# A graph-network layer on one core: two small elementwise steps move from VectorE to ScalarE

## The chip, the cores and the metric

The kernel runs on one core of one Trainium2 chip. The metric is device time in microseconds (us) of that core for one launch, the median of a few runs. A core has five engines with a queue of instructions each: TensorE (PE, with its weight loads shown apart as PEld), VectorE (DVE), ScalarE (ACT), GpSimd (POOL) and SyncE (SP, which here issues nearly all DMAs). An engine takes its own queue in order; a wait for another engine is a wait on a semaphore. Where an instruction has more waits than fit into it, the surplus stands before it in the queue as EVENT_SEMAPHORE instructions.

## The reference, cut to what matters

```python
# N = 12500 nodes, 412500 edges sorted by dst; idx_i = src, idx_j = dst
h   = maximum(layernorm(x), 0)
h1  = h @ W_in2f                                         # 128 -> 128
Wij = (ssp(f_ij @ W_f1 + b_f1) @ W_f2 + b_f2) * rcut[:, None]
agg = segment_sum(h1[idx_j] * Wij, idx_i)                # one message per edge
out = x + ssp(agg @ W_o1 + b_o1) @ W_o2 + b_o2           # ssp = softplus - log 2
```

The call of the inner function passes `src` as `idx_i` and `dst` as `idx_j`: rows are gathered by `dst`, which is sorted, and summed by `src`, which is not.

## The kernel before, in words

**Main loop.** The edges are cut into chunks of 512 (806 chunks of four tiles of 128 edges); four chunks make a group. One pass of the loop (`step(k)`) works on several chunks at once, each at another stage; the whole order of instructions is written out by hand under `tc.manual_schedule()`. For one chunk the stages are:

- `rows`: SP loads 32 rows of the node table near the chunk's first `dst` (L608).
- `hidden`, for two chunks at a time: TensorE makes the filter's first layer `z` (L653); ScalarE takes abs (L656), exp (L657) and, one step later, log (L662) of it; `hidden_end` on VectorE makes `r` from `z` and the log (L668).
- `bias` and `value`: ScalarE writes the second layer's bias over a PSUM bank `v` (L757) and TensorE adds the second layer's products to it (L764, `start=False`).
- `window` and `pick`: VectorE compares to make the 0/1 matrix `at` (L744), and TensorE multiplies it with the loaded rows (L772); that is the gather. `picked`: ScalarE scales the result by the edge weights into `hg`, tile by tile (L780).
- `blocks`, `rank`, `rank_end`: VectorE (L673), TensorE (L692, L725) and VectorE again (L697) find a free slot in a DRAM table for every edge.
- `message`: VectorE multiplies `v` by `hg` into `o` (L791), and GpSimd scatters the four tiles of `o` into their slots by indirect DMAs (L795).

A row of `o` has 129 columns: 128 message values and, in the last column, the edge's place within its block of 128 nodes. `o` is a tile for two chunks (8 rows of 129 per partition), with four buffers. At every even chunk, before the product of that chunk, one VectorE instruction copies the 8 places per partition into the last column of both chunks (L789):

```python
if c % 2 == 0:
    kept["o"] = quad.tile([P, 2 * QT, RW], F32, name="o", bufs=4)
    w = min(2, self.n - c) * QT
    nc.vector.tensor_copy(kept["o"][:, :w, P], self.place[:, c * QT:c * QT + w])
```

As the first writer of a buffer that was used before, this copy carries the waits for the eight indirect DMAs that last read the buffer.

In an even step ScalarE's order is: bias `v` of chunk k+2 (which waits for the product L791 of chunk k, whose PSUM bank it takes), the four `hg` of chunk k+1, abs and exp for the pair k+4. In an odd step it is: bias `v`, four `hg`, log. VectorE's order in an even step is: `r` of the pair k+2 (which waits for the log of the step before), `at`, the copy of the places, the product L791, then the rank's reduction and the comparisons.

**Collecting.** The edges are in 7 segments with a slot table each. Behind the loop's front the slots of a finished segment are read back (`Collect`): SP loads them as `m` (L833, five buffers), VectorE compares the last column with 0..127 into `to` (L844), TensorE multiplies `m` by `to` and sums in PSUM (L857), and the sum is added to `agg` in SBUF (L878, L880). From about 2460 us on this runs beside the main loop.

**Tail.** The last segment is collected after the loop, and the output network runs with it, four blocks of nodes (a quad) at a time, 25 quads. `finish` is a generator with a stage per `yield`: 0, SP loads `x` into `xo` (L410, six buffers); 1, TensorE makes `z_out` (L414), ScalarE takes abs, relu, exp and log (L385, L386, L394, L395); 2, VectorE adds the two parts (`r_out`, L420) and adds `b_o2` to `xo` (L423); 3, TensorE makes the last product `v_out` (L427) in a PSUM bank of tag `v` (three buffers); 4, VectorE adds it to `xo` (L431); 5, SP stores `xo` (L434). While the quad q is collected, the quads q+1, q-1, q-2, q-3 and q-4 take one stage each, in that order. The same function also serves a fallback path that these inputs do not take.

Of the kernel before, what the change touches and what calls it, by code (L numbers as in the profile page):

```python
# [9 lines left out]
F32 = mybir.dt.float32  # L10
# [3 lines left out]
AF = mybir.ActivationFunctionType  # L14
# [3 lines left out]
P = 128  # L18
# [3 lines left out]
QT = CH // P  # L22
# [19 lines left out]
def gnn_kernel(  # L42
# [20 lines left out]
    nc = tc.nc  # L63
# [52 lines left out]
    def sbuf(name, shape, dtype=F32):  # L116
        return const.tile(shape, dtype, name=name)

    def spread(t, n):
        return t[:, None, :].to_broadcast([t.shape[0], n, P])  # L120
# [9 lines left out]
    for q in range(NQ):  # L130
        start = max(0, q * QN - NEAR)
        tables.append((start, (q + 1) * QN + NEAR + P - start))
    table_of = []
    for c in range(NC):
        n = c * CH * N // n_edges
# [4 lines left out]
    win, wf1, wf2, wo1, wo2 = (sbuf(n, [P, P]) for n in ("win", "wf1", "wf2", "wo1", "wo2"))  # L140
    bf1, nbf1, bo1 = (sbuf(n, [P, 1]) for n in ("bf1", "nbf1", "bo1"))
    bf2, bo2 = (sbuf(n, [P, P]) for n in ("bf2", "bo2"))
# [240 lines left out]
    def softplus_parts(a, r, z, bias):  # L383

        nc.scalar.activation(a, z, AF.Abs, bias=bias)  # L385
        nc.scalar.activation(r, z, AF.Relu, bias=bias)  # L386
# [6 lines left out]
    def softplus_logs(a):  # L393
        nc.scalar.activation(a, a, AF.Exp, scale=-1.0)  # L394
        nc.scalar.activation(a, a, AF.Ln, bias=half, scale=0.5)  # L395

    def finish(t0, n, sT, quad, psum):


        n0 = t0 * P  # L400
        full = min(n, N // P - t0)
        rest = N - n0 - full * P if full < n else 0
        xo = quad.tile([P, QT, P], F32, name="xo", bufs=6)
        pieces = []
        if full:
            pieces.append((P, slice(0, full), slice(n0, n0 + full * P)))
        if rest:
            pieces.append((rest, slice(full, n), slice(n0 + full * P, N)))
        for p, cs, rows in pieces:
            nc.sync.dma_start(xo[:p, cs, :], x[rows, :].rearrange("(c p) f -> p c f", p=p))  # L410
        yield

        z = psum.tile([P, 2, CH], F32, name="z_out", tag="z")[:, 0, :n * P]
        nc.tensor.matmul(z, wo1, sT, start=True, stop=True)  # L414
        a_n = quad.tile([P, 2, CH], F32, name="a_out", tag="a", bufs=2)[:, 0, :n * P]
        r_n = quad.tile([P, 2, CH], F32, name="r_out", tag="r", bufs=3)[:, 0, :n * P]
        softplus_parts(a_n, r_n, z, bo1)
        softplus_logs(a_n)
        yield
        nc.vector.tensor_add(r_n, r_n, a_n)  # L420
        for p, cs, rows in pieces:
            xi = xo[:p, cs, :]
            nc.vector.tensor_add(xi, xi, spread(bo2[:p, :], xi.shape[1]))  # L423
        yield
        v = psum.tile([P, QT, P], F32, name="v_out", tag="v", bufs=3)
        for i in range(n):
            nc.tensor.matmul(v[:, i, :], r_n[:, i * P:(i + 1) * P], wo2, start=True, stop=True)  # L427
        yield
        for p, cs, rows in pieces:
            xi = xo[:p, cs, :]  # L430
            nc.vector.tensor_add(xi, xi, v[:p, cs, :])  # L431
        yield
        for p, cs, rows in pieces:
            nc.sync.dma_start(out[rows, :].rearrange("(c p) f -> p c f", p=p), xo[:p, cs, :])  # L434


    def anyway(edge, quad, psum):
# [67 lines left out]
        for t0 in range(0, NTILE, QT):  # L505
            n = min(QT, NTILE - t0)
            o = quad.tile([P, QT, P], F32, name="s_out")
            nc.sync.dma_start(o[:, :n, :], sums[t0 * P:(t0 + n) * P, :].rearrange("(c p) f -> p c f", p=P))
            tps = psum.tile([P, QT, P], F32, name="t_out", tag="nodes")
            for i in range(n):  # L510
                nc.tensor.transpose(tps[:, i, :], o[:, i, :], ident)
            sT = quad.tile([P, QT, P], F32, name="sT")
            nc.scalar.activation(sT[:, :n, :], tps[:, :n, :], AF.Copy)
            for _ in finish(t0, n, sT[:, :n, :].rearrange("p c f -> p (c f)"), quad, psum):
                pass


    with tc.tile_pool(name="edge", bufs=2) as edge, tc.tile_pool(
        name="quad", bufs=3
# [3 lines left out]
        kept = {}  # L523
# [41 lines left out]
        class Group:  # L565
# [218 lines left out]
            def message(self, c, v, hg):  # L784

                if c % 2 == 0:
                    kept["o"] = quad.tile([P, 2 * QT, RW], F32, name="o", bufs=4)
                    w = min(2, self.n - c) * QT
                    nc.vector.tensor_copy(kept["o"][:, :w, P], self.place[:, c * QT:c * QT + w])  # L789
                o = kept["o"][:, c % 2 * QT:(c % 2 + 1) * QT, :]  # L790
                nc.vector.tensor_mul(o[:, :, :P], v, hg)  # L791
                views = self.seg.views
                for i in range(QT):
                    j = c * QT + i
                    put = nc.gpsimd.indirect_dma_start(  # L795
                        out=views[j % VIEWS],
                        out_offset=bass.IndirectOffsetOnAxis(ap=self.slot[:, j:j + 1], axis=0),
                        in_=o[:, i, :],
                        in_offset=None,
                    )  # L800
                    if i == 0 and self.g * NCHUNK + c == self.seg.cleared:
                        for name in self.seg.clears:
                            tc.add_manual_dep(
                                put.ins, name,
                                mybir.DependencyInfo(mybir.DependencyClass.Sync,
                                                     mybir.DependencyReason.DATA),
                                reason="cleared slots")
# [189 lines left out]
        t0, i = 0, 0  # L997
        while i < len(segs):

            j = max(range(i, len(segs)), key=lambda j: sum(todo[i:j + 1]) / (due[j] - t0))  # L1000
            n = sum(todo[i:j + 1])
            for m in range(n):
                zeros.setdefault(t0 + m * (due[j] - t0) // n, []).append(clears.pop(0))
            t0, i = due[j], j + 1
# [5 lines left out]
        while len(rate) < len(at):  # L1010
            n = len(at) - len(rate)
# [13 lines left out]
        i, k = 0, todo[0][0]  # L1025
# [43 lines left out]
        with tc.manual_schedule():  # L1069
# [49 lines left out]
            outs = []  # L1119
            for b in range(0, NBLK, QT):  # L1120
                n = min(QT, NBLK - b)
                sT = kept["agg"][:, b:b + n, :].rearrange("p c f -> p (c f)")
                outs.append(finish(b, n, sT, quad, psum))

            def go(q):
                if 0 <= q < NQ:
# [31 lines left out]
    with tc.If(missed > 0):  # L1158
        with tc.tile_pool(name="any_e", bufs=2) as edge, tc.tile_pool(
            name="any_q", bufs=2  # L1160
# [51 lines left out]
```

## Time and profile before

| | |
|---|---|
| runs of the kernel before | 5771.6, 5732.79, 5770.01 us; median 5770.01 |
| the profiled execution | 5772.48 us, of which 5770.8 us is the span of its instructions |
| mean granted TensorE clock | 0.718 of full speed; about 0.6 from 200 to 2500 us, about 0.8 from 2500 to 5620 us, 0.94 after |
| busy share of the span | PE 67%, DVE 59%, POOL 54%, ACT 47% |
| copy of the places (L789, DVE) | 403 instructions of 166 ns, 66.8 us |
| `b_o2` added to `xo` (L423, DVE) | 26 instructions, 16.9 us |
| main loop | from the start to about 5620 us |
| tail | about 5620 to 5765 us, then the last stores |

The busy shares are shares of the whole span and overlap each other; no engine is busy all the time. Durations of single instructions overlap with their neighbours on the same engine, so that the step from one start to the next is less than the duration. "Idle before" is the time in which an engine stood still ahead of an instruction, and after "<-" stands what ended it; "remote" means that the profile names no instruction for it, and "issue" that it shows no wait. The clock is the share of full speed that TensorE was granted.

### The profile page before, as it was taken

How to read it: one execution, taken by the hardware profiler on the slowest of the kernel's cores; microseconds unless marked ns; L12 is line 12 of the kernel's file. 1: busy time of each engine (PE TensorE's matmuls, PEld its weight loads, DVE VectorE, ACT ScalarE, POOL GpSimd, SP SyncE). 2: the span in 40 equal slices, each digit the busy share in tenths (PEclk: the TensorE clock that was granted, in tenths of full speed). 3: DMA queues.
4: the chain of work that ended last, by engine and by line, in shares of the span. 5: the costliest groups of instructions: out<-in, count | busy, mean ns of one | idle time of the engine just before them, and what ended most of it. 6: DMA issues, size and time to landing. Idle time of an engine off the chain costs nothing. (4 is left out here: it accounts for less than half of the span.)

```text
span 5770.8 us, 71871 instructions
## 1 busy us (share of the span) xinstructions
PE 3877.3 (67%) x21576; PEld 2912.2 (50%) x21576; DVE 3382.9 (59%) x6726; ACT 2715.3 (47%) x5490; POOL 3103.5 (54%) x3244
## 2 busy tenths in 40 slices
PE   5556555556555555577777777777777777777778
PEld 3333333333333333356655666566566665655557
DVE  5555555555444444466665666666666666566767
ACT  4455554555444444444444444444444444444444
POOL 5555555555555555555555555555555555555550
PEclk7665566565556566578777787788877788787879
DMA  5444443343333333255664554655555555555547
GB/s 150 138 135 141 130 141 119 115 137 104 99 89 87 106 109 87 82 152 161 188 183 137 158 160 144 190 163 157 160 168 173 154 150 178 165 141 153 145 126 215
DMA packets 515581, 820.80 MB, mean 142 GB/s; under 512 B 177074, under 2 KB 312870, under 8 KB 515186
## 3 DMA queue, kind: packets, MB, share of 16 engines
q1 hardware_dynamic: 411586, 602.85, 37.4%
q0 software_dynamic: 103168, 213.15, 11.2%
q8 instruction: 176, 2.88, 0.2%
q14 instruction: 219, 1.79, 0.1%
q10 hardware_dynamic: 432, 0.13, 0.0%
HBM read 419.09 MB, written 396.64 MB: 141 GB/s over the span
## 5 line engine op out<-in xcount | busy, mean ns | idle before, releaser
L795 POOL DMA_INDIRECT slots<-o,slot x3224 | 3100.3, 962 | 2522.6 <-DVE o L791 1605.2
L764 PE MATMUL v<-wf,r 128*128 128x128 f32 x6448 | 1209.4, 345 | 527.4 <-ACT a L657 207.3
L857 PEld LDWEIGHTS acc<-to,m 128*128 128x128 f32 x8132 | 1249.1, 238 | 577.1 <-issue 280.8
L857 PE MATMUL acc<-to,m 128*128 128x128 f32 x8132 | 1342.0, 329 | 271.0 <-DVE agg L880 136.4
L764 PEld LDWEIGHTS v<-wf,r 128*128 128x128 f32 x6448 | 1077.6, 251 | 850.7 <-issue 301.8
L780 ACT ACTIVATE hg<-picked,rcut 128x128 f32<-128x128 f32 x3224 | 913.1, 365 | 1256.6 <-remote 801.2
L697 DVE TENSOR_REDUCE top<-free 128x4 f32<-128x392 f32 x806 | 451.5, 560 | 1650.5 <-remote 990.2
L757 ACT ACTIVATE v<-bf 128x512 f32<-128x512 f32 x804 | 478.0, 595 | 1212.9 <-DVE o L791 888.5
L653 PE MATMUL z<-f,wf 20*128 20x512 f32 x1612 | 661.1, 881 | 406.9 <-DVE r L668 242.4
L844 DVE TENSOR_TENSOR to<-count_ps,m 128x512 f32<-128x512 f32 (+3 forms) x824 | 644.7, 806 | 255.3 <-remote 109.3
L772 PE MATMUL picked<-near,at 96*128 96x128 bf16 x3224 | 398.5, 257 | 495.3 <-ACT hg L780 317.4
L668 DVE SCALAR_TENSOR_TENSOR r<-z,nbf,a 128x1024 f32<-128x1024 f32 x403 | 516.2, 1281 | 242.3 <-ACT a L662 136.3
L656 ACT ACTIVATE a<-z,bf 128x1024 f32<-128x1024 f32 x403 | 454.0, 1127 | 400.4 <-remote 267.8
L772 PEld LDWEIGHTS <-at 96*128 96x128 bf16 x3224 | 315.5, 118 | 558.1 <-issue 531.3
L791 DVE TENSOR_TENSOR o<-v,hg 128x512 f32<-128x512 f32 x806 | 547.8, 680 | 16.8 <-ACT hg L780 12.8
L744 DVE TENSOR_TENSOR at<-count_ps,rel 96x512 bf16<-96x512 f32 x806 | 545.3, 677 | 0.0
L653 PEld LDWEIGHTS z<-f,wf 20*128 20x128 f32 x1612 | 174.6, 241 | 620.9 <-issue 428.9
L662 ACT ACTIVATE a<-a,half 128x1024 f32<-128x1024 f32 x403 | 468.1, 1162 | 0.0
L673 DVE TENSOR_TENSOR inb<-count_ps,blk 128x392 f16<-128x392 f32 x806 | 445.9, 554 | 0.0
L657 ACT ACTIVATE a<-a 128x1024 f32<-128x1024 f32 x403 | 425.8, 1057 | 12.8
L725 PE MATMUL free<-inb,rest_of 128*128 128x392 f16 x806 | 335.3, 416 | 117.6 <-issue 46.9
L692 PE MATMUL free<-inb,after 128*128 128x392 f16 x806 | 335.9, 417 | 17.4 <-issue 13.6
(108 smaller groups left out, 1142.5 us busy)
## 6 DMA issues: line engine op xcount, KB each, us to landing
m<-slots SPq DMA_DIRECT2D x311, 387.0 KB
m<-slots SPq DMA_DIRECT2D x317, 258.0 KB
rel<-rel_d SPq DMA_DIRECT2D x202, 384.0 KB
m<-slots SPq DMA_DIRECT2D x172, 322.5 KB
slots<-o,slot POOLq DMA_INDIRECT x3224
slots<-zero SPq DMA_DIRECT2D x96, 387.0 KB
slots<-zero SPq DMA_DIRECT2D x64, 516.0 KB
f<-in_f_t SPq DMA_DIRECT2D x404, 80.0 KB
```

The source lines that it names most:

```text
L653: nc.tensor.matmul(z[:, k, :], wf1[rows, :], self.f[rows, :], start=True, stop=True)
L662: nc.scalar.activation(a, a, AF.Ln, bias=half, scale=0.5)
L668: nc.vector.scalar_tensor_tensor(r, z, nbf1, a, op0=ALU.max, op1=ALU.add)
L744: nc.vector.tensor_tensor(at, prow_ps.to_broadcast([WP, CH]), self.rel[:, c, :], op=ALU.is_equal)
L757: nc.scalar.activation(v, spread(bf12, QT), AF.Copy)
L764: nc.tensor.matmul(v[:, i, :], r[:, i * P:(i + 1) * P], wf2, start=False, stop=True, skip_group_check=True)
L772: nc.tensor.matmul(ps[:, i, :], at[:, i * P:(i + 1) * P], near, start=i == 0, stop=i == QT - 1, skip_group_check=True)
L780: nc.scalar.activation(hg[:, i, :], ps[:, i, :], AF.Copy, scale=self.rcut[:, j:j + 1])
L791: nc.vector.tensor_mul(o[:, :, :P], v, hg)
L795: put = nc.gpsimd.indirect_dma_start(out=views[j % VIEWS], out_offset=bass.IndirectOffsetOnAxis(ap=self.slot[:, j:j + 1], axis=0), in_=o[: ...
L844: nc.vector.tensor_tensor(to[:, :n, :], count_ps[:, None, :].to_broadcast([P, n, P]), self.m[u][:, :n, P:].to_broadcast([P, n, P]), op=ALU ...
L857: nc.tensor.matmul(self.acc[b // QT][:, i, :], m[:, j, :P], to[:, j, :], start=t == 0, stop=t == self.seg.tiles(b) - 1)
```

## The change

The copy of the places into the last column of `o` becomes a ScalarE activation (a plain copy) at the same place of the source. In the tail, ScalarE writes `b_o2`, repeated for every node of the quad, over the PSUM bank `v_out` in stage 2, and the last product is added onto it (`start=False`); the VectorE addition of `b_o2` to `xo` is left out there. The bank is so taken one stage earlier. The fallback path keeps the old form (`seeded=False`).

```diff
-    def finish(t0, n, sT, quad, psum):
+    def finish(t0, n, sT, quad, psum, seeded=False):
...
         nc.vector.tensor_add(r_n, r_n, a_n)
-        for p, cs, rows in pieces:
-            xi = xo[:p, cs, :]
-            nc.vector.tensor_add(xi, xi, spread(bo2[:p, :], xi.shape[1]))
+        v = psum.tile([P, QT, P], F32, name="v_out", tag="v", bufs=3)
+        if seeded:
+            nc.scalar.activation(v[:, :n, :], spread(bo2, n), AF.Copy)
+        else:
+            for p, cs, rows in pieces:
+                xi = xo[:p, cs, :]
+                nc.vector.tensor_add(xi, xi, spread(bo2[:p, :], xi.shape[1]))
         yield
-        v = psum.tile([P, QT, P], F32, name="v_out", tag="v", bufs=3)
         for i in range(n):
-            nc.tensor.matmul(v[:, i, :], r_n[:, i * P:(i + 1) * P], wo2, start=True, stop=True)
+            nc.tensor.matmul(v[:, i, :], r_n[:, i * P:(i + 1) * P], wo2, start=not seeded,
+                             stop=True, skip_group_check=seeded)
...
                 if c % 2 == 0:
                     kept["o"] = quad.tile([P, 2 * QT, RW], F32, name="o", bufs=4)
                     w = min(2, self.n - c) * QT
-                    nc.vector.tensor_copy(kept["o"][:, :w, P], self.place[:, c * QT:c * QT + w])
+                    nc.scalar.activation(kept["o"][:, :w, P],
+                                         self.place[:, c * QT:c * QT + w], AF.Copy)
...
-                outs.append(finish(b, n, sT, quad, psum))
+                outs.append(finish(b, n, sT, quad, psum, seeded=True))
```

In the built program the order of instructions on TensorE, GpSimd and SyncE is the same as before. ScalarE has 403 copies more, 388 of them directly ahead of an even step's bias `v` (L757; 14 others have one evacuation, L878, between), and 25 writes of `v_out`. VectorE has these 403 and the 26 additions fewer. The waits for the eight indirect DMAs stand at ScalarE's copy now, and on VectorE they stand at the product L791 that follows. The first indirect DMA of a pair waits for ScalarE's copy as well as for the product, and the first `v_out` product of a quad waits for ScalarE's write.

## The prediction

> **What bounds the kernel now.** I read the page's shares first, then the waits, then the time line of two kinds of pair (two chunks, which share one log, one `r` and one tile `o`), then the tail.
>
> ```profile
> PE 3877.3 (67%) x21576; PEld 2912.2 (50%) x21576; DVE 3382.9 (59%) x6726; ACT 2715.3 (47%) x5490; POOL 3103.5 (54%) x3244
> PEclk7665566565556566578777787788877788787879
> ```
>
> No engine is busy all the time, so the main loop is set by a chain of waits. The clock row gives the granted TensorE clock in 40 slices: about 0.6 before collecting starts at 2460 us, about 0.8 after.
>
> ```profile
> POOL slots L795 <- DVE o L791: 1605.2, 358, 25.4
> DVE top L697 <- remote: 990.2, 163, 12.1
> ACT v L757 <- DVE o L791: 888.5, 325, 9.0
> ACT hg L780 <- remote: 801.2, 152, 10.2
> ```
>
> The columns are total us, times and longest. ScalarE's bias `v` waits 888 us for VectorE's product L791, and so does GpSimd (1605 us, so its scatters follow and do not lead). "remote" is a wait with no named releaser: VectorE and ScalarE stand there for rank and gather products of TensorE whose completion is signalled late. Pairing each rank reduction L697 with the recorded end of its product L692, 410 of 806 begin over 3 us after it, 2534 us in sum.
>
> ```profile
> 1799.26 1.16 ACT L662 ACTIVATE a<-a,half 128x1024 f32<-128x1024 f32 x1
> 1800.45 1.28 DVE L668 SCALAR_TENSOR_TENSOR r<-z,nbf,a 128x1024 f32<-128x1024 f32 x1 [2.35 <-issue]
> 1801.65 0.68 DVE L744 TENSOR_TENSOR at<-count_ps,rel 96x512 bf16<-96x512 f32 x1
> 1802.25 0.16 DVE L789 COPY o<-place 128x8 f32<-128x8 f32 x1
> 1802.32 0.68 DVE L791 TENSOR_TENSOR o<-v,hg 128x512 f32<-128x512 f32 x1
> 1803.04 0.60 ACT L757 ACTIVATE v<-bf 128x512 f32<-128x512 f32 x1 [2.62 <-issue]
> ```
>
> Columns: start, duration, engine, line, [idle before]. This is the end of a pair without a late TensorE signal. `r` starts 0.03 us after the log, `at` 1.20 later, the copy 0.60 later, the product 0.07 later, and the bias starts 0.04 us after the product ends, having stood idle 2.62 us. From the product at 1793.37 to the one at 1802.32 the starts on the chain differ by 0.71 (to bias), 0.54 (to `hg`), 1.00 (to abs), 1.16 (to exp), 0.96 (to bias), 0.52 (to `hg`), 1.00 (to log), 1.19 (to `r`), 1.20, 0.60 and 0.07: 8.95 us. By the starts of the 403 copies the mean pair takes 13.89 us; the fastest repeat this 8.95, many others before 2460 us take about 18.8, and in those the surplus of some 10 us is the "remote" wait.
>
> **The change, part by part.**
>
> ```profile
> L789 DVE COPY o<-place 128x8 f32<-128x8 f32 x403 | 66.8, 166 | 0.0
> L757 ACT ACTIVATE v<-bf 128x512 f32<-128x512 f32 x804 | 478.0, 595 | 1212.9 <-DVE o L791 888.5 <-issue 306.2 <-DVE at L744 17.1
> L333 ACT ACTIVATE rs<-rs 128x4 f32<-128x4 f32 x24 | 4.9, 205 | 0.8
> L423 DVE TENSOR_TENSOR xo<-xo,bo 128x512 f32<-128x512 f32 x24 | 16.4, 685 | 0.0
> ```
>
> (Count | busy us, mean ns | idle before.)
>
> *The copy leaves VectorE.* Its duration is 166 ns, 66.8 us in all, but the product starts 69 to 70 ns after the copy in all 403 cases, and `at` to copy is 597 ns, the same as `at` to product in odd steps. So the copy occupies 0.07 us of the chain: 403 x 0.07 = 28 us at most. The eight scatter waits move to the product behind `at`. They were surplus instructions of up to 50 ns, four to a copy, and the 597 ns show that they ran under `at`; there they still run. If that cover went, 4 x 0.05 = 0.2 us a pair, 80 us, would appear on VectorE; it does not go, since `at` stays ahead of them. The copy never found VectorE idle, so the buffers' scatters had always landed.
>
> *The copy joins ScalarE.* No row shows this shape on ScalarE. The nearest is L333, 128x4, at 205 ns; the far one is a bias, 595 ns. I take 0.2 us, plus four surplus waits at 38 ns (the median of those ahead of L357), 0.35 us. It stands ahead of the even step's bias (L757), and behind it wait the four `hg`, abs and exp, then TensorE's `value` and `z` products. Work that hides it: `r`, `at` and the product, 1.87 us from the start of `r` to that of the product, in which ScalarE waits anyway. By the trace's starts, ScalarE was idle 2.13 us or more ahead of 394 of 402 even biases. Cost 0. The other end, all of it exposed: 403 x 0.35 = 141 us.
>
> In the Trainium skill, ScalarE: Activation LUTs, section "Rules for kernel authors", speaks against the change: simple elementwise work (it names relu, max, min, add and mul) belongs on VectorE. The same page, section "What ACT_TABLE_LOAD costs", gives 186 ns + 0.833 ns per element, 193 ns here, close to the 205 ns row and to the biases' 595. By that rule, if ScalarE set the pace, the move would cost an estimated 403 x 0.19 = 77 us; the idle time ahead of the biases says that it costs nothing.
>
> *GpSimd.* The first scatter of a pair waits for the copy too, one surplus wait of 17 ns (median of the 832 there). The copy starts right after the log, over 1 us ahead of the product for which the scatter waits anyway: 403 x 0.017 = 7 us on GpSimd, beside 1605 us of idleness. Cost 0.
>
> *How much of the 28 us arrives.* `r` starts within 0.1 us of the log's end in 282 of 403 pairs, and the bias right after the product nearly always, so the 0.07 us reach ScalarE. What may swallow them is a late TensorE signal. If its lateness moves along with the work, all 28 us arrive. If it ends at a time of its own, only pairs without it gain: 145 of 402 pairs are under 12 us, 145 x 0.07 = 10 us. I take the middle, 19; with every wait set elsewhere it would be 0.
>
> *The tail.*
>
> ```profile
> 5677.12 0.69 DVE L880 TENSOR_TENSOR agg<-agg,acc 128x512 f32<-128x512 f32 x1
> 5677.73 0.69 DVE L420 TENSOR_TENSOR r_out<-r_out,a_out 128x512 f32<-128x512 f32 x1
> 5678.33 0.68 DVE L423 TENSOR_TENSOR xo<-xo,bo 128x512 f32<-128x512 f32 x1
> 5678.94 0.69 DVE L844 TENSOR_TENSOR to<-count_ps,m 128x512 f32<-128x512 f32 x1
> 5679.54 0.68 DVE L431 TENSOR_TENSOR xo<-xo,v_out 128x512 f32<-128x512 f32 x1
> 5680.13 0.68 DVE L844 TENSOR_TENSOR to<-count_ps,m 128x512 f32<-128x512 f32 x1
> ```
>
> One quad, 3.74 us from `agg` to `agg`: six VectorE instructions 0.60 apart, the third of them the `b_o2` addition that goes. TensorE's starts in the same quad: z to `v_out` 0.86, from there to the sum's sixteen products 0.89, and 1.99 for these, although eight take 0.90 where nothing waits: the second eight wait for the fourth VectorE row. Without the third row VectorE needs 3.14, and TensorE's own 0.86 + 0.89 + 2 x 0.90 = 3.55 decides: 0.19 less a quad, and over 24 quads at most 4.6 us. But from the seventh quad on SP holds the pace:
>
> ```profile
> SPq L410 <- DMA out<-xo: 39.0, 19, 4.4
> ```
>
> The load of `xo` waits for the store six quads before, and the loads of `m` queue behind it. SP's stores begin at 5688.08, 5691.91, 5696.15 and 5700.35, 4.1 us apart, more than VectorE's 3.74, and from 5714 us on VectorE waits for `m`. So only some five quads gain, 5 x 0.19 = 1 us. ScalarE's writes of `v_out` cost 25 x 0.6 = 15 us, at the price of the bias row (same shape, same bank type). Per quad ScalarE has 0.69 + 0.68 + 0.63 + 0.72 less overlap, 2.5 us of 3.74, so 0.6 fits in its wait for z. The bank was read by L431 an iteration earlier. In the drain after 5757 us nothing covers: log, then two writes (2 x 0.55) come ahead of the last products, while VectorE loses its two additions: the end moves by +1 us. If all 24 quads' gain came, and nothing in the drain, the tail would be 4.6 us shorter; if the writes lay open, 14 us longer. I take -1 + 1 = 0.
>
> **The sum.** Own time 5772.5 (span 5770.8 and 1.7 around it) - 19 + 0 = 5753.5. The median of the runs is 2.5 us lower than the profiled execution: 5751.
>
> **The rivals.**
>
> *Everything is swallowed.* The late signals decide; 28 us vanish in the waits for TensorE. For it: 2534 us of lateness and a mean pair of 13.89 against a chain of 8.95. Against it: the 8.95 and 18.8 us pairs contain the same tight piece from log to bias. Time: 5770, no change.
>
> *More late signals (slower).* Place: the rank and gather products; price: 2534 / 410 = 6.2 us each. The work on ScalarE and VectorE is re-timed by the change, and the alternation of 8.95 and 18.8 us pairs shows that the lateness depends on how the work falls. Five more late chunks of 806 (0.6%) eat the gain, and from 13 on the kernel is slower by over 1%; twenty (5% more) give 5751 + 124 = 5875, fourteen 5838. Against it: TensorE's, GpSimd's and SP's orders are the same, and nothing is added to TensorE. What makes the lateness I cannot name from this profile.
>
> *Fewer late signals.* The same lever the other way: ten fewer give 5751 - 62 = 5689.
>
> *ScalarE's copy lies open.* 141 - 28 = +113, 5883; it needs the 2.13 us of idleness to fall below 0.35. Nothing here does that.
>
> *It does not do what it says.* VectorE could still hold a wait for the copy; the built order shows none on the product.
>
> **How the numbers follow.** Most of the gain arrives: 0.50, at 5751, with its own range 5735 to 5768 (0 to 28 us, tail 5 either way). Swallowed: 0.23, 5755 to 5785. More late signals: 0.14; fewer: 0.10; open copy: 0.03. One per cent, 58 us, is about what a measurement of this kernel can tell from no change: its three runs lie 39 us apart. Faster by over 1% needs fewer late signals: 0.09. Slower by over 1% comes from most of the third case and the open copy: 0.14. Within 1%: 0.77. The range cuts off half of the two tail cases: 5700 to 5820.
>
> **What would show it.** The copy as 403 ScalarE rows of about 0.2 us with ScalarE still idle over 1.5 us between them and the even bias; `at` to product 0.60 us in even steps as in odd ones; fastest pairs of 8.88 us instead of 8.95; the `xo`, `bo` rows gone in the tail and its quads still near 3.6 to 4.2 us. I am wrong if the even bias no longer starts right at the product's end, if VectorE's product waits for scatters, or if the waits on "remote" and the count of late rank reductions move by more than 3%.

## The result, and the profile after

The changed kernel is slower: 5804.95 us median (5780.48 to 5821.42, 8 runs) against 5745.6 us for the kernel before (5704.52 to 5771.6, 8 runs). The ratio is 1.0102, its 95% interval 1.0077 to 1.0126. The forecast was a gain of some 0.3%. The profiled execution took 5803.15 us, 5801.4 of it span.

The busy shares and the clock row hardly move; VectorE has lost some 43 us of work and ScalarE has gained 55:

```profile
PE 3835.5 (66%) x21576; PEld 2881.8 (50%) x21576; DVE 3339.8 (58%) x6297; ACT 2769.9 (48%) x5918; POOL 3098.7 (53%) x3244
PEclk7565656656666555678777877778777787777879
```

The waits have the same heads, with one new name on the first (total us, times, longest):

```profile
POOL slots L801 <- ACT v L762: 1237.7, 265, 26.0
DVE top L702 <- remote: 951.5, 140, 12.3
ACT v L762 <- DVE o L797: 861.7, 330, 9.6
ACT hg L785 <- remote: 851.9, 144, 10.4
```

GpSimd's scatters seem to wait for ScalarE's bias. They do not: the wait they gained is for ScalarE's copy, which is over long before. The label goes by the last ScalarE instruction ahead of the scatter. The time line (start, duration, engine, line, [idle before]) of the end of a pair shows the chain as forecast:

```profile
1366.22 1.16 ACT L667 ACTIVATE a<-a,half 128x1024 f32<-128x1024 f32 x1
1367.26 0.22 ACT L794 ACTIVATE o<-place 128x8 f32<-128x8 f32 x1
1367.42 1.28 DVE L673 SCALAR_TENSOR_TENSOR r<-z,nbf,a 128x1024 f32<-128x1024 f32 x1 [0.59 <-ACT a L667]
1368.62 0.68 DVE L749 TENSOR_TENSOR at<-count_ps,rel 96x512 bf16<-96x512 f32 x1
1369.21 0.68 DVE L797 TENSOR_TENSOR o<-v,hg 128x512 f32<-128x512 f32 x1
1369.92 0.60 ACT L762 ACTIVATE v<-bf 128x512 f32<-128x512 f32 x1 [2.44 <-DVE o L797]
```

The copy (1367.26) sits right behind the log, `at` to product is 0.59 us with nothing between, and the bias starts 0.03 us after the product, having stood idle 2.44 us. The fastest pairs take 8.88 us. What is new stands in another pair, at the scatter:

```profile
1550.36 0.68 DVE L797 TENSOR_TENSOR o<-v,hg 128x512 f32<-128x512 f32 x1
...
1551.07 0.60 ACT L762 ACTIVATE v<-bf 128x512 f32<-128x512 f32 x1 [2.44 <-DVE o L797]
...
1551.78 0.96 POOL L801 DMA_INDIRECT slots<-o,slot  x1 [8.18 <-ACT v L762]
```

The same place in the kernel before:

```profile
1793.37 0.68 DVE L791 TENSOR_TENSOR o<-v,hg 128x512 f32<-128x512 f32 x1
...
1794.33 0.96 POOL L795 DMA_INDIRECT slots<-o,slot  x1 [7.72 <-DVE o L791]
```

After the change the product ends at 1551.04 and the first scatter starts at 1551.78, 0.74 us later; before, the product ends at 1794.05 and the scatter starts 0.28 us later. I call this distance the scatter lag. Its median in even chunks was 0.28 us before and is 0.75 us after; in odd chunks, whose first scatter has two waits as before, the shortest is 0.28 us in both kernels. In the built program the first scatter of a pair waits for an earlier scatter and for VectorE before, with VectorE's wait on the scatter itself; after, it has ScalarE's as a third, and VectorE's has moved into an EVENT_SEMAPHORE ahead of it, so that the scatter is taken up only when that has been resolved.

In the tail the `xo`, `bo` rows are gone and the quads are shorter where the forecast had them shorter:

```profile
5706.25 0.69 DVE L886 TENSOR_TENSOR agg<-agg,acc 128x512 f32<-128x512 f32 x1 [0.43 <-PE acc L863]
...
5708.07 0.69 DVE L436 TENSOR_TENSOR xo<-xo,v_out 128x512 f32<-128x512 f32 x1
...
5709.79 0.69 DVE L886 TENSOR_TENSOR agg<-agg,acc 128x512 f32<-128x512 f32 x1 [0.43 <-PE acc L863]
```

3.54 us from `agg` to `agg` instead of 3.74. The loss is in the main loop: up to the last product the profiled execution is 35 us longer than before.

### The profile page after: what moved, and what is told of

The parts are those of the page before. It is cut to its first block, busy times and chain, and to the rows that moved or that the text cites. A ratio compares the mean times of both kernels' runs of the same rounds, so it can differ in the third digit from the quotient of the medians.

```text
span 5801.4 us, 73471 instructions
## 1 busy us (share of the span) xinstructions
PE 3835.5 (66%) x21576; PEld 2881.8 (50%) x21576; DVE 3339.8 (58%) x6297; ACT 2769.9 (48%) x5918; POOL 3098.7 (53%) x3244
## 4 chain that ended last, share of the span: by engine, by line
## 5 line engine op out<-in xcount | busy, mean ns | idle before, releaser
L769 PE MATMUL v<-wf,r 128*128 128x128 f32 x6448 | 1196.5, 343 | 508.7 <-issue 181.8
L863 PEld LDWEIGHTS acc<-to,m 128*128 128x128 f32 x8132 | 1228.0, 235 | 608.4 <-issue 341.2
L863 PE MATMUL acc<-to,m 128*128 128x128 f32 x8132 | 1320.8, 325 | 306.4 <-issue 153.1
```

Of the source, the lines that this page charges most:

```text
L769: nc.tensor.matmul(v[:, i, :], r[:, i * P:(i + 1) * P], wf2, start=False, stop=True, skip_group_check=True)
L863: nc.tensor.matmul(self.acc[b // QT][:, i, :], m[:, j, :P], to[:, j, :], start=t == 0, stop=t == self.seg.tiles(b) - 1)
```

## The experiments

**What could do it.** Theory 1: the third wait delays GpSimd by 0.47 us per pair, and GpSimd's burst of scatters does lead. Theory 2: ScalarE's copy itself costs. Theory 3: with the chain 0.07 us shorter the work falls otherwise and TensorE's results come later. Theory 4: the tail's part costs. The runs came in five groups, on chips that the record numbers 5, 0, 15, 9 and 15 again. The kernel before took 4227 to 4234 us in the groups on 5 and 9 and in the second one on 15 (called condition B here), 5749 us in the group on 0 (condition A; it fits the first measurement), and 5820 us in the first group on 15 (condition C), 25 minutes before the second. So number 15 stands on both sides: that the chip makes the difference is not shown, and what sets the condition is open. The expectations below speak of chips where this text speaks of conditions. Ratios are to the kernel before in the same group.

### In condition B: nothing counts but GpSimd

Only the first part of the change, `places_only`:

```diff
-                    nc.vector.tensor_copy(kept["o"][:, :w, P], self.place[:, c * QT:c * QT + w])
+                    nc.scalar.activation(kept["o"][:, :w, P],
+                                         self.place[:, c * QT:c * QT + w], AF.Copy)
```

> Only the places move to ScalarE; the tail is as before. Theory 1 (the first scatter of a pair, which now has a third wait, starts 0.75 us after the product instead of 0.28, and GpSimd's burst sets the loop): scatter lag 0.75 us in even chunks, fastest pair 8.88 us, time 1.010 to 1.013 of before, that is about 5800 to 5820 us. Theory 2 (ScalarE's copy with its waits delays ScalarE): the same time, so this run does not tell 1 from 2. Theory 3 (the work is merely re-timed and TensorE's late signals fall otherwise): anything from 0.99 to 1.01. Theory 4 (the loss sits in the tail's new bank and ScalarE's writes): 0.995 to 1.000.

Only the second part, `bias_only` (the diff of `finish` and its call, with VectorE's copy kept):

> Only b_o2 goes into the PSUM bank; VectorE keeps the copy of the places. Theories 1, 2 and 3: scatter lag 0.28 us, fastest pair 8.95 us, tail after the last product some 4 us shorter, time 0.998 to 1.000 of before. Theory 4: 1.008 to 1.012.

The changed kernel with a wait more on VectorE, `product_waits`:

```diff
-                    nc.scalar.activation(kept["o"][:, :w, P],
+                    kept["placed"] = nc.scalar.activation(kept["o"][:, :w, P],
...
-                nc.vector.tensor_mul(o[:, :, :P], v, hg)
+                product = nc.vector.tensor_mul(o[:, :, :P], v, hg)
+                if c % 2 == 0:
+                    tc.add_manual_dep(product.ins, kept["placed"].ins.name, ...)
```

> As the changed kernel, but VectorE's even product also waits for ScalarE's copy (long done by then), so that the scatter behind the product no longer needs a wait of its own for it: two waits instead of three. Theory 1: scatter lag back at 0.28 us, fastest pair 8.88 us, time 0.993 to 0.998 of before, about 5710 to 5735 us, below both kernels. Theory 2: ScalarE's work is that of the changed kernel, so 1.008 to 1.012. Theory 3: no relation to the lag, 0.99 to 1.01; it is favoured if the lag is 0.28 us and the time still near 1.01.

The kernel before with the third wait alone, `third_wait`:

```diff
                     nc.vector.tensor_copy(kept["o"][:, :w, P], self.place[:, c * QT:c * QT + w])
+                    dummy = quad.tile([P, 2 * QT], F32, name="dummy", bufs=4)
+                    kept["placed"] = nc.scalar.activation(
+                        dummy[:, :w], self.place[:, c * QT:c * QT + w], AF.Copy)
...
+                    if i == 0 and c % 2 == 0:
+                        tc.add_manual_dep(put.ins, kept["placed"].ins.name, ...)
```

> As before (VectorE copies the places), with a ScalarE copy of the same size into a tile that nobody reads, for which the first scatter of a pair waits: three waits on it. Theory 1: scatter lag 0.75 us, fastest pair 8.95 us, time 1.010 to 1.018 of before, 5803 to 5850 us, since the 0.07 us on VectorE stay. Theory 2: the dummy copy carries no waits for scatters and lies in ScalarE's idle time, so 1.000 to 1.004. Theory 3: 0.99 to 1.01, with no order between the four runs by their scatter lag.

Measured: 0.9999 (0.9989 to 1.0008), 1.0005 (0.9996 to 1.0014), 0.9998 (0.9989 to 1.0007) and 1.0000 (0.9991 to 1.0009). None of the theories had reckoned with such a condition. The page of `places_only`:

```profile
PE 3371.5 (80%) x21576; PEld 2594.6 (61%) x21576; DVE 3347.3 (79%) x6323; ACT 2752.4 (65%) x5893; POOL 3105.6 (73%) x3244
PEclk8776767666666666589999999999999989999999
L796 POOL DMA_INDIRECT slots<-o,slot x3224 | 3102.5, 962 | 1011.6 <-issue 771.5
```

GpSimd's row has 1011.6 us of idle time, nearly all of it the 0.30 us behind each scatter; waits for products are at most 54 us of it. In the median GpSimd trails the products by 25 us. Its scatters start 1.266 us apart, 3224 x 1.266 = 4082 us, and that is the main loop; the mean pair takes 10.09 us, eight scatters. There the 0.07 us and the 0.47 us both lie behind GpSimd's backlog. Rank reductions for which VectorE stands idle over 1 us and that come over 3 us after the recorded end of their product do not occur in any profile of condition B; those of A and C have 222 to 252 each.

### In condition A: the third wait costs, and so does the change without it

> The changed kernel itself, beside the kernel before on the same chip. In the four runs above the kernel before took 4227 us, not 5746, and GpSimd trailed the products by 10 to 30 us: there GpSimd sets the loop with 3224 scatters 1.266 us apart, 4081 us. If this chip is like that one: 0.999 to 1.001, since a start that is 0.47 us late lies behind the backlog. If it is like the first one (GpSimd runs dry, the pairs alternate between some 9 and 19 us): 1.008 to 1.013, scatter lag 0.75 us in even chunks.

> As the run product_waits. On a chip where GpSimd never runs dry: 0.999 to 1.001. On a chip like the first one, theory 1 (the third wait): 0.993 to 0.998, scatter lag 0.28 us; theory 2 (ScalarE's copy): 1.008 to 1.012; theory 3 (re-timing): 0.99 to 1.01 without relation to the lag.

> As the run third_wait. On a chip where GpSimd never runs dry: 0.999 to 1.001. On a chip like the first one, theory 1: 1.010 to 1.018, scatter lag 0.75 us; theory 2: 1.000 to 1.004; theory 3: 0.99 to 1.01 without relation to the lag.

`pool_between` is the kernel before with a GpSimd instruction more, at the place where the first scatter has just been issued:

```diff
+                    if i == 0 and c % 2 == 0:
+                        idle = quad.tile([P, 64], F32, name="idle", bufs=4)
+                        nc.gpsimd.memset(idle, 0.0)
```

> As before, with one GpSimd memset of a 128x64 tile that nobody reads between the first and the second scatter of every pair, so GpSimd's burst is longer by the memset's step, estimated at 0.1 to 0.5 us. If GpSimd sets the loop (by its backlog, or on the first chip by what follows its burst), the time grows by 403 such steps, 40 to 200 us; the step is to be read from the trace and the growth divided by it. If GpSimd only follows, as the prediction had it: 0.999 to 1.001.

| run | ratio (95% interval) | scatter lag, even, median | fastest pair | first product to 177th even one | from there to the last even one |
|---|---|---|---|---|---|
| before (first measurement's profile) | 1 | 0.28 us | 8.95 us | 2387 us | 3198 us |
| after_again | 1.0109 (1.0075 to 1.0143) | 0.75 | 8.88 | 2414 | 3238 |
| product_waits_2 | 1.0092 (1.0063 to 1.0120) | 0.28 | 8.88 | 2376 | 3248 |
| third_wait_2 | 1.0152 (1.0122 to 1.0183) | 0.75 | 8.95 | 2433 | 3187 |
| pool_between | 1.0000 (0.9977 to 1.0022) | 0.28 | 8.95 | 2378 | 3191 |

The last two columns come from one profile each, and the executions of the kernel before differ by up to 67 us, so only their large differences count. (After's first profile has 2416 and 3202.)

`third_wait_2` bears out theory 1 in its size: 403 x 0.47 = 189 us of later starts, of which 1.5%, 87 us on 5749, reach the end. The profile shows the delay as time of the event semaphore (count, shortest/median/longest ns):

```profile
L798 POOLq EVENT_SEMAPHORE  x833: 17/43/16053, 29.3 to 5650.7; - x167
```

16 us is a wait for a product; in the kernel before the longest there was 43 ns, as it is in `product_waits_2`, whose scatter has two waits:

```profile
L795 POOLq EVENT_SEMAPHORE  x832: 17/17/43, 35.5 to 5614.4; - x167
L807 POOLq EVENT_SEMAPHORE  x832: 17/17/43, 35.3 to 5652.5; - x167
```

But `product_waits_2` is slow all the same. Theory 1 is true and not enough: with the third wait taken out, the changed kernel does not get measurably faster (1.0092 against 1.0109). Its two stages part company: up to the 177th pair, about where collecting begins, it is as fast as before or faster (2376); what it loses, it loses after.

Why GpSimd counts at all shows in the pairs. Before collecting, pairs of 8.95 and of some 18.8 us alternate, and two such pairs have a nearly fixed length together (I say that they lock): 27.77 us for the two before, 27.64 in `product_waits_2`, but 28.15 and 28.12 in the two profiles of after and 28.18 in `third_wait_2`. The two pairs with one late start of GpSimd in them are 0.4 to 0.5 us longer, the 0.47 us of the lag. After collecting begins a second pattern is frequent, single pairs of about 16.4 us. One of `product_waits_2` (time line):

```profile
3077.84 0.68 DVE L797 TENSOR_TENSOR o<-v,hg 128x512 f32<-128x512 f32 x1
...
3078.80 0.96 POOL L807 DMA_INDIRECT slots<-o,slot  x1 [6.54 <-DVE o L797]
...
3085.48 0.33 PE L697 MATMUL free<-inb,after 128*128 128x392 f16 x1
...
3087.64 0.96 POOL L807 DMA_INDIRECT slots<-o,slot  x1 [0.30 <-issue]
3090.22 1.14 ACT L785 ACTIVATE hg<-picked,rcut 128x128 f32<-128x128 f32 x4 [4.68 <-remote]
3090.26 0.57 DVE L702 TENSOR_REDUCE top<-free 128x4 f32<-128x392 f32 x1 [6.86 <-remote]
...
3094.23 0.68 DVE L797 TENSOR_TENSOR o<-v,hg 128x512 f32<-128x512 f32 x1
```

From product to product 16.39 us. GpSimd is dry (it has no scatter to do and stands idle 6.54 us), scatters eight tiles from 3078.80 to 3088.60, and then runs dry again; the rank's product was recorded at 3085.48, but VectorE's reduction of it starts 4.4 us after its end, at 3090.26, and ScalarE, which waits for the gather product, goes on at 3090.22: both 1.6 us after GpSimd's last scatter. A pair of this kind in the changed kernel, with the third wait:

```profile
3097.22 0.68 DVE L797 TENSOR_TENSOR o<-v,hg 128x512 f32<-128x512 f32 x1
...
3098.65 0.95 POOL L801 DMA_INDIRECT slots<-o,slot  x1 [6.96 <-ACT v L762]
...
3107.49 0.96 POOL L801 DMA_INDIRECT slots<-o,slot  x1 [0.30 <-issue]
3109.97 1.14 ACT L785 ACTIVATE hg<-picked,rcut 128x128 f32<-128x128 f32 x4 [7.69 <-remote]
...
3113.97 0.68 DVE L797 TENSOR_TENSOR o<-v,hg 128x512 f32<-128x512 f32 x1
```

GpSimd starts 1.43 us after the product instead of 0.96, its burst ends 0.47 later, and ScalarE is released 0.37 us later, at 12.75 us after the product instead of 12.38; the pair takes 16.75. TensorE has no wait for a scatter in the program. Yet in all profiles of before, after, `third_wait_2`, `product_waits_2` and `dve_early_only` together, of some 840 late rank reductions that found GpSimd dry, one came more than 3.2 us after the end of its burst. (VectorE stood idle over 1 us ahead of each of these; some 360 more such reductions came while GpSimd was at work.) That TensorE's results follow the burst is read from this coincidence; no run here shows what ties them to it.

Counting the single-pair pattern after the 177th pair (16.2 to 16.6 us; 16.7 to 16.95 with the third wait): 24 before, 22 in `pool_between`, 45 in `product_waits_2`, 16 and 18 in the two profiles of after, 14 in `third_wait_2`. The mean pair of before takes 13.89 us, so 22 more pairs of 16.4 are 22 x 2.5 = 55 us, about what `product_waits_2` lost there. Counted in both windows of length together, the difference is smaller: 51 such pairs in `product_waits_2`, 34 before, 32 in `pool_between`, 23 to 27 with the third wait. This is a reading of single profiles; it says where the time is, not why 0.07 us makes the pattern more frequent.

`pool_between` tells nothing: its memset of 0.17 us fits into the 0.30 us behind a scatter and lengthens that step from 1.266 to 1.280 us only, 403 x 0.014 = 6 us.

### In condition C: which 0.07 us

```diff
                     nc.vector.tensor_copy(kept["o"][:, :w, P], self.place[:, c * QT:c * QT + w])
+                    dummy = quad.tile([P, 2 * QT], F32, name="dummy", bufs=4)
+                    nc.scalar.activation(dummy[:, :w], self.place[:, c * QT:c * QT + w], AF.Copy)
```

> As before, with a ScalarE copy of 128x8 per pair into a tile that nobody reads, at the place where the changed kernel has its copy; nobody waits for it and it waits for no scatter. What the last four runs left open: product_waits_2 has its scatter lag back at 0.28 us and still took 1.009, so the third wait is not all. Theory 2 (the ScalarE copy itself costs): 1.005 to 1.010, with scatter lag 0.28 us. Theory 1 (the third wait alone, 0.47 us a pair): 0.999 to 1.002. Theory 3 (taking 0.07 us off VectorE's chain packs TensorE's work closer and what comes after 2460 us suffers): 0.999 to 1.002.

The second leaves ScalarE alone and moves VectorE's copy:

```diff
                 if c % 2 == 0:
-                    kept["o"] = quad.tile([P, 2 * QT, RW], F32, name="o", bufs=4)
-                    w = min(2, self.n - c) * QT
-                    nc.vector.tensor_copy(kept["o"][:, :w, P], self.place[:, c * QT:c * QT + w])
+                    kept["o"] = kept.pop("next_o")
...
             for r in ready:
                 for _ in r:
                     pass
+            if k % 2 and has(k + 1):
+                of(k + 1)[0].places(of(k + 1)[1])      # the three lines above, into next_o
```

> The copy of the places stays on VectorE, but at the end of the odd step, behind the rank's reduction and ahead of the next comparisons, off the stretch from log to product; scatter with two waits. Fastest pair 8.88 us, scatter lag 0.28 us. Theory 1 and theory 2: all of the gain and none of the cost, 0.994 to 0.999. Theory 3: 1.005 to 1.010, as in product_waits_2, since the chain loses the same 0.07 us.

> Only b_o2 in the PSUM bank. Theories 1 to 3: 0.998 to 1.001. Theory 4 (the tail part costs after all, or shifts something in the loop): 1.005 to 1.010.

```diff
+                    if i == 0 and c % 2 == 0:
+                        idle = quad.tile([P, 1032], F32, name="idle", bufs=1)
+                        nc.gpsimd.memset(idle, 0.0)
```

> As before, with a GpSimd memset of a 128x1032 tile that nobody reads (0.96 us in its one row of before) between the first and the second scatter of every pair; the smaller memset fitted into the gap of 0.3 us that follows a scatter and made the step only 0.014 us longer. Estimated 0.8 us more for each pair's burst. If GpSimd's burst leads in the pairs that alternate between 9 and 19 us: two pairs 27.7 plus 1.6, 29.3 us, and the time 1.010 to 1.055, up to 403 x 0.8 = 320 us. If GpSimd only follows: 0.999 to 1.003.

| run | ratio (95% interval) | late rank reductions (> 3 us), sum | to 177th even product | after |
|---|---|---|---|---|
| act_dummy | 1.0018 (0.9993 to 1.0042) | 419, 2551 us | 2396 us | 3243 us |
| bias_only_2 | 1.0014 (0.9988 to 1.0040) | 431, 2586 | 2398 | 3224 |
| dve_early_only | 1.0109 (1.0070 to 1.0147) | 439, 2631 | 2404 | 3312 |
| pool_long | 0.9659 (0.9612 to 0.9706) | 362, 2465 | 2343 | 3093 |

Theory 4 falls: the tail's part costs nothing that can be measured. So does theory 2, in two steps. A copy more on ScalarE costs nothing measurable (`act_dummy`); that copy carries no waits for scatters, but the one in `product_waits_2` does, and there no copy kept ScalarE waiting over 0.15 us, and between the copy and the even bias ScalarE is still idle 2.44 us in the median and at least 0.75 in the 388 pairs in which the two are neighbours.

`dve_early_only` has no third wait, nothing on ScalarE and no change in the tail. It takes 0.07 us off the stretch from log to product (fastest pair 8.88 us), and it loses 1.1%, nearly all after collecting begins. It has 50 of the 16.4 us pairs there, against 34 and 23. But that is not all it does. At the copy's new place the waits for the eight scatters often lie open:

```profile
3403.46 0.17 DVE L721 TENSOR_SCALAR slot<-top 128x16 int32<-128x16 f32 x1
3403.83 0.18 DVE L787 COPY o<-place 128x8 f32<-128x8 f32 x1 [0.20 <-issue]
3403.91 0.56 DVE L673 TENSOR_TENSOR inb<-count_ps,blk 128x392 f16<-128x392 f32 x1
```

In the kernel before:

```profile
1790.35 0.17 DVE L721 TENSOR_SCALAR slot<-top 128x16 int32<-128x16 f32 x1
1790.43 0.56 DVE L673 TENSOR_TENSOR inb<-count_ps,blk 128x392 f16<-128x392 f32 x1
```

From `slot` to the instruction behind the copy it takes 0.45 us in the median of the 202 pairs in which the copy follows `slot`, where the kernel before has 0.08; in most others, behind the long reduction, 0.08 us is added. So this run alone does not isolate the 0.07 us. What it has in common with `product_waits_2`, where VectorE has no such open waits, is the shorter stretch, and both lose about 1%: the step that was to bring the gain goes with a loss in conditions A and C, as theory 3 allowed. Why it does so is not shown.

`pool_long` is the surprise. The memset takes 0.98 us and the step around it 2.095 instead of 1.266, 0.83 us a pair, 334 us of GpSimd's time, for nothing, and the kernel is 3.4% faster. A burst that is longer should have made the locked pairs longer by as much, had GpSimd's end alone led; instead the patterns are broken up: after the 177th pair GpSimd is dry (idle over 0.5 us) ahead of two successive pairs 72 times, against 160 to 192 in `pool_between` and the other three kernels of this table. The late results themselves still keep their distance from the burst's end. Behind a lone burst of eight scatters, 0.83 us longer here, the eight late rank reductions that found GpSimd dry start 0.06 to 0.11 or 1.52 to 1.57 us after the end; in the kernel before, 31 of 44 start 0.11 to 0.22 or 1.49 to 1.66 us after it.

### Two more groups, again in condition B

```diff
                     nc.vector.tensor_copy(kept["o"][:, :w, P], self.place[:, c * QT:c * QT + w])
+                    for _ in range(1):        # chain_4: range(4)
+                        dummy = quad.tile([P, 2 * QT], F32, name="dummy", bufs=4)
+                        nc.vector.tensor_copy(dummy[:, :w], self.place[:, c * QT:c * QT + w])
```

> As before, with one more VectorE copy of 128x8 per pair, into a tile that nobody reads, right behind the copy of the places and ahead of the even product: the stretch that the change makes 0.07 us shorter is made 0.07 us longer. Scatter lag 0.28 us, fastest pair 9.02 us. Theory 3 in its directed form (a shorter chain packs TensorE's work closer and its completions come later, so a longer one helps): 0.985 to 0.996. Theory 3 without direction (any re-timing moves the time, to either side): 0.99 to 1.015. If only the chain's length counted, as the prediction had it: 1.002 to 1.005.

> As chain_1 with four such copies: 0.28 us longer, fastest pair 9.23 us. Directed form: 0.96 to 0.99, more than chain_1. Without direction: 0.98 to 1.02. Chain's length alone: 1.01 to 1.02.

> The changed kernel with the GpSimd memset of pool_long (0.83 us more between the first and the second scatter of a pair). If the change's loss and the memset's gain act apart: 0.966 x 1.010, 0.976. If the loss comes from the rhythm in which GpSimd runs dry, which the memset breaks up: 0.960 to 0.970, the change costing nothing or gaining there.

> As before, with the memset in both chunks of a pair, 1.66 us more on GpSimd per pair: 8 x 1.266 + 1.66 = 11.8 us of work for a mean pair that took 13.9. If slower scatters help by spreading the work: below pool_long, 0.93 to 0.966. If pool_long broke one rhythm only: 0.966 to 1.0. If GpSimd's burst leads after all: above 1.0.

> As chain_1. On a chip where GpSimd never runs dry (before near 4230 us): 0.999 to 1.001 again. On a chip like the first: directed form of theory 3 (shorter chain, later completions) 0.985 to 0.996; without direction 0.99 to 1.015; chain's length alone 1.002 to 1.005.

> As chain_4. On a chip where GpSimd never runs dry: 1.006 to 1.009 again, since 0.28 us on the chain brings it near GpSimd's pace. On a chip like the first: directed form 0.96 to 0.99; without direction 0.98 to 1.02; chain's length alone 1.01 to 1.02.

Measured: `chain_1` 1.0006 (0.9997 to 1.0016) and again 1.0019 (1.0009 to 1.0028); `chain_4` 1.0074 (1.0061 to 1.0088) and 1.0064 (1.0050 to 1.0078); `after_pool_long` 1.0794 (1.0779 to 1.0809); `pool_long_2` 1.1586 (1.1570 to 1.1602). In this condition they only confirm who leads: one memset costs 336 us, where 403 x 0.83 = 334, and two cost 670, where 806 x 0.83 = 669. `chain_4` costs 0.7%, since its fastest pair of 9.24 us leaves less below GpSimd's 10.1. So the memset that gains 3.4% in condition C loses 7.9% here: no version for use comes out of it. Whether a longer chain helps in A or C, and whether the change still costs 1% beside the memset there, stays open.

## Why the prediction was wrong

*The copy leaves VectorE: right to the hundredth.* 8.88 us, `at` to product 597 ns, the waits hidden under `at`.

*The copy joins ScalarE at no cost: right.* 227 ns in the median of 403 instead of the 0.2 us taken, idle time ahead of the even bias still 2.44 us in the median, and `act_dummy` measures the price at 1.0018, an interval that holds 1. The Trainium skill's page ScalarE: Activation LUTs, section "Rules for kernel authors", which spoke against such a move, fits the sign of the result but not its place: the estimate of 77 us that the prediction worked out was for a ScalarE that sets the pace, and in the trace ScalarE is idle ahead of the even bias as before; the loss goes with GpSimd's third wait and with VectorE's shorter chain. Two counts of the prediction were slightly off, without effect on its sum: the copy took 0.07 us in 400 of the 403 pairs and 0.11 us in three, and ScalarE was idle 2.1 us or more ahead of 391 of 402 even biases.

*GpSimd at cost 0: the first step that failed.* It was priced as one more instruction of 17 ns, and hidden on the ground that GpSimd stood idle 1605 us, "so its scatters follow and do not lead". The wait that was added was long satisfied, but it displaced the wait that mattered from the scatter to an instruction ahead of it, and the scatter came 0.47 us later, 28 times the price. And the idle time was no cover: it is the gap between bursts, and the late results of TensorE that find GpSimd dry come within some 3 us of a burst's end, and 0.37 us later in the pair shown whose burst ends 0.47 us later. By itself the wait costs 1.5% (`third_wait_2`).

*How much of the 28 us arrives: the second.* The bounds were 28 and 0, on the argument that a late signal either moves with the work or ends at a time of its own. The case that a shorter chain makes lateness more frequent was left out there; it came in only as the rival "more late signals", at 0.14 and with nothing named that would bring it about. `product_waits_2` and `dve_early_only` measure it at 0.9 and 1.1%, with 434 and 439 late reductions (the second kernel with the open waits told above): against 410 and 411 in the profiles of before and `pool_between`, and 419 and 431 in `act_dummy` and `bias_only_2`. That is the sign of that rival, at half its price or less (it put twenty more late chunks at 124 us, and 49 and 71 us were lost); the lateness in sum grew by about what was lost, from 2534 to 2581 us and from 2551 and 2586 to 2631. But the rival's own count did not rise in the changed kernel: 384 and 405. There the third wait makes fewer chunks late and the locked pairs longer.

*The two losses do not add up.* 1.5% and 0.9% were measured apart, 1.0% together. In the loop as it runs in conditions A and C the effects of these edits do not sum from parts, so no sum of the prediction's kind would have found them. The measured 5805 us lies inside the stated range of 5700 to 5820; that is luck, since the range was drawn from cases of late signals and has no term for GpSimd's wait. The kernel before came out at 5745.6 us, 24 us below the three runs from which the prediction started.

*The tail at 0: right.* Its early quads went to 3.54 us, as reckoned from TensorE's 3.55; later ones are irregular around 4 us as before; and the drain from the last `agg` to the end grew from 13.1 to 14.4 us, the +1. `bias_only` and `bias_only_2` hold 1 in their intervals.

*What was to show it wrong.* The remote wait on the rank reduction fell from 990 to 952 us and the late ones from 410 to 384, while ScalarE's remote wait ahead of `hg` rose from 801 to 852, all by more than 3%; so that test spoke, but the first two point to a gain. It asked for the lateness of chunks and not for the length of the pairs.

**What stays open.** Why TensorE's results come late in conditions A and C and not in B. It is not the granted clock alone: for 3083.0 to 3088.6 us of the pair shown, the profile grants 0.95, and the results are late all the same; and before collecting the clock is 0.61 of full speed in both kernels and 0.68 in B, 10% apart, while the mean pair takes 13.6 and 10.0 us. The Trainium skill's page TensorE: Matmul & The Clock Gate, section "Seeing it yourself", warns that the recorded clock events can be unreliable and that a quarter of the clock has been seen to stick for over 50 us. No run here shows such a stuck clock, and the semaphore events kept in the traces speak against it as the cause.

These events show when an engine's signal of finished work arrived. In every profile of B, 99% of TensorE's signals come within 0.03 us of the recorded end of the work. In every one of A and C half of them come over 0.3 us, and a tenth over 3.2 us, after the last recorded end ahead of them; 99% of ScalarE's and VectorE's signals, as far as they are recorded, come within 0.02 us in all three conditions. And TensorE's late signals come in batches: in the pair of `product_waits_2` shown above, five arrive between 3090.14 and 3090.44 us, for work that by the record ended between 3085.25 and 3087.82 (the profile models these ends). A TensorE that worked more slowly than recorded would hand its results over one by one. Batches of four or more, each signal within 0.15 us of the one before, occur 191 to 214 times in each profile of A and C but that of `pool_long`, which has 139, and 1 to 4 times in each of B; the 214 are those of `product_waits_2` and `dve_early_only`. So what is late there is the signal and not TensorE's pace. What holds it back, and what makes it part of one condition and not of another, stays open.

## What to carry to other kernels

An added wait is not only its own instruction: look at which wait it pushes off the instruction and into the queue ahead, above all on GpSimd's indirect DMAs, and let an engine that already waits for the same source carry it; here that brought the lag back to 0.28 us, though not the time. Idle time is cover only if the engine's next burst does not set the rhythm; check whether what comes late elsewhere ends with that burst. Where the profile is full of unnamed waits and of pairs that lock to a few lengths, take gains of 0.1 us a pair as unsigned, and measure in more than one group of runs, each with the kernel before beside it, before believing a per cent.

## What the runs showed that was not expected

The same program took 4227, 5749 and 5820 us in three groups of runs, and on chip number 15 both 5820 and, 25 minutes later, 4234 us. A 128x8 copy on ScalarE takes 216 to 227 ns. A third wait on an indirect DMA of GpSimd, which moves the wait that ends last off the instruction, adds 0.47 us between the end of what it waits for and its start (0.28 to 0.75). TensorE's signals can arrive in batches, microseconds after the recorded end of the work. A GpSimd memset of 0.17 us behind an indirect DMA costs 0.014 us, one of 0.98 us costs 0.83. And 0.83 us a pair of useless work on GpSimd made the kernel before 3.4% faster in condition C, and the changed kernel 7.9% slower in condition B, where the change alone costs nothing.
